# A gather's wait for TensorE's queries, at every third group of edges instead of every second

## The chip, the cores and the metric

The kernel runs on one core of one Trainium2 chip. The metric is device time in microseconds (us) of one execution: the median of several runs. Five engines work side by side, each on its own list of instructions: TensorE (PE in the profile; its weight loads are PEld), VectorE (DVE), ScalarE (ACT), GpSimd (POOL) and SyncE (SP). They wait for each other by semaphores: an instruction that is done raises a count, and another one waits until the count is high enough.

## The reference, cut to what matters

A graph has 12,500 nodes with 128 numbers each and 200,000 edges, in the order of their target node `dst`. Two convolutions with four heads follow a layer norm. In each, node projections give a query `q`, a key `k` and a value `v`, and then for all edges:

```
kj = k[src] + e
vj = v[src] + e
alpha = jnp.einsum('ehc,ehc->eh', q[dst], kj) / jnp.sqrt(...)
p = jnp.exp(alpha - amax[dst])
w = p / denom[dst]
out = jax.ops.segment_sum((vj * w[..., None]).reshape(-1, H * C), dst, num_segments=n)
```

A third stage multiplies gathered node rows by numbers of the edge and sums them by target. What matters here: an edge's key and value are fetched from the row of its source node, which lies anywhere, and its query comes from its target node, which lies close to that of the edge before.

## The kernel before, in words

**Work.** The edges are cut into 391 groups of 512 (4 tiles of 128). Each convolution runs over all groups, so 782 groups in all. `conv` (L775) writes the order out by hand: a loop over steps `s`, in which different parts of the work are done for different groups, and every engine gets its instructions in exactly that order.

**One step.** In step `s` the parts that matter are these, in the order of the code:

- `fetch_kv(s + 3)` (L814): GpSimd issues four indirect DMAs, one for each 128 edges, through `gather` (L597; the DMA itself is at L602). Each reads 128 rows of key and value (1 KB each) into the tile `kv`. There are 20 such tiles (`LAG + KVS`). Nothing else runs on GpSimd in the convolutions.
- `turn(s + 2)` and `keep_sums` (ScalarE: tile `OT` at L850 and L852; the sums `acc` at L867).
- `messages` and `sum_up` for a group 15 steps back (VectorE L839 and L840; TensorE L862 and L860). `messages` is the last reader of that group's `kv` tile.
- `scores(s)` (VectorE L883, L885 and L887): it multiplies TensorE's queries, tile `pq`, by the keys in `kv`.
- `query(s + 1)` (TensorE, L823): eight matmul instructions (four in the code) into two banks of `pq`. Four banks rotate, and the node work takes some of the same banks in between.

So each engine can run ahead of the others only as far as these buffers let it. TensorE's query of a group needs banks that `scores` of an earlier group has read; `scores` needs TensorE's result for its own group.

**The wait.** The first of a group's four gathers may get one more wait, by `gather`'s argument `behind`: it waits until the last matmul of `query(g - 3)` has raised TensorE's semaphore. `asked[g - 3]` holds that matmul. The data doesn't need it. In the code before, every odd group has this wait, 194 groups of each convolution (there is no `asked` for a negative number). All other waits of a gather are about data: the `kv` tile must have been read (`messages` of group g - 20), and the gather eight places earlier must have landed.

The third stage has gathers of its own (tile `hg`, the same L602) with a wait of its own kind; it isn't part of the change.

Of the kernel before, what the change touches and what calls it, by code (L numbers as in the profile page):

```python
# [533 lines left out]
def sorted_path(ctx: ExitStack, tc: tile.TileContext, sh_: Shared, x, edge_attr, out):  # L534
# [33 lines left out]
    kv_d, q_d, s1_d = sh_.kv_d, sh_.q_d, sh_.s1_d  # L568
# [30 lines left out]
    def gather(t, rows, g, behind=None):  # L599

        for u in range(U):
            i = nc.gpsimd.indirect_dma_start(  # L602
                out=t[:, u, :], out_offset=None, in_=rows[:, :],
                in_offset=bass.IndirectOffsetOnAxis(ap=srcI[:, g * U + u:g * U + u + 1], axis=0))
            if behind is not None and u == 0:
                tc.add_manual_dep(i.ins, behind.ins.name, mybir.DependencyInfo(
                    mybir.DependencyClass.Sync, mybir.DependencyReason.DATA), reason="a pause for TensorE's results")
# [169 lines left out]
    def conv(li):  # L777
# [8 lines left out]
        pps, outs, msgs, pas, asked = {}, {}, {}, {}, {}  # L786
# [4 lines left out]
        qws, kvs, Os, OTs, pqs, ALs, segs, accs, bst = {}, {}, {}, {}, {}, {}, {}, {}, {}  # L791
# [22 lines left out]

        def fetch_kv(g):
            kvs[g] = pool.tile([P, U, 2 * D], F32, name="kv", bufs=LAG + KVS)
            gather(kvs[g], kv_d[li], g, asked.get(g - 3) if g % 2 else None)

        def query(g):
            pqs[g] = [bank().rearrange("p (u c) -> p u c", u=2) for _ in range(U // 2)]  # L820
# [191 lines left out]
        with tc.manual_schedule():  # L1012
            for s in range(-AHEAD, last):
# [34 lines left out]
                if 0 <= s + 3 < NGR:  # L1048
                    fetch_kv(s + 3)
# [624 lines left out]
```

## Time and profile before

| what | value |
|---|---|
| median of 3 runs | 7359.88 us (7340.25 to 7360.03) |
| the profiled execution | 7424.75 us; its span, first to last instruction, 7422.9 us |
| granted TensorE clock, mean | 0.792 of full speed |
| first convolution, first gather to last message | 137.5 to about 2568 us |
| second convolution | about 2594 to 5030 us |
| third stage | 5057 us to the end |
| POOL busy in the span | 4867.4 us (66%) |
| PE, DVE, ACT busy | 5031.8 (68%), 4923.4 (66%), 3053.5 (41%) us |
| mean share of the 16 DMA engines, 700 to 2300 us | 0.56 to 0.63 |
| issues of `kv` gathers | 3128 (782 groups of 4) |

The profile records when each instruction started and ended on its engine, and how long the engine stood idle before it. Of that idle time it says what ended it ("releaser"), as far as a semaphore's update was recorded. About a fifth of TensorE's updates are missing, so many waits end on "remote". The ends of matmuls are modelled, not observed. Four views are used here: the page of sums, the list of waits (who waited for whom, in total, number of times, longest), the instructions of one tile, and the timeline (instructions in order of their start).

### The profile page before, as it was taken

The numbers are of one execution on the slowest core, as the hardware profiler recorded it, in microseconds if no ns is written. First come the engines' busy times: TensorE is split into PE (matmuls) and PEld (weight loads), VectorE is DVE, ScalarE is ACT, GpSimd is POOL, SyncE is SP. The second block draws the span as 40 slices with busy tenths as digits, with TensorE's granted clock in tenths as the row PEclk, the third lists the DMA queues.
The fourth block names the chain that finished last, engine by engine and source line by source line (L and its number), as shares of the span: only waits on it lengthen the run. The fifth ranks groups of instructions, "written<-read, shape, count | busy, mean of one in ns | idle before, by whom it ended". The sixth has DMA issues, their size and how long they took to land.

```text
span 7422.9 us, 89199 instructions
## 1 busy us (share of the span) xinstructions
PE 5031.8 (68%) x21249; PEld 3219.3 (43%) x21250; DVE 4923.4 (66%) x13362; ACT 3053.5 (41%) x7785; POOL 4867.4 (66%) x4779
## 2 busy tenths in 40 slices
PE   5566666666777646665666666665777787777777
PEld 4454555555555444444454545452233333333332
DVE  5566666777777746666676777774566666666666
ACT  3333333333333223333444444443555555555554
POOL 6676667676666367767666776654566666666664
PEclk8677777787777867777777777777888888888888
DMA  6455555566666445555555555544455555555554
GB/s 186 135 149 150 148 158 160 162 167 164 168 177 174 129 134 138 143 143 143 146 152 152 153 156 160 157 135 121 125 137 142 144 145 147 149 149 151 152 153 116
DMA packets 868134, 1107.31 MB, mean 149 GB/s; under 512 B 143858, under 2 KB 631568, under 8 KB 867603
## 3 DMA queue, kind: packets, MB, share of 16 engines
q0 software_dynamic: 250240, 692.16, 34.6%
q1 hardware_dynamic: 615832, 408.51, 19.8%
q8 instruction: 176, 2.88, 0.2%
q14 instruction: 355, 2.91, 0.1%
q10 hardware_dynamic: 1531, 0.84, 0.0%
HBM read 935.35 MB, written 165.60 MB: 148 GB/s over the span
## 4 chain that ended last, share of the span: by engine, by line
PE 27%; DVE 22%; another core or an unknown queue 17%; issue 15%; POOL 7%; ACT 6%; DMA 3%; SPq 1%; DVEq 0%; POOLq 0%; ACTq 0%
PE pa L862 8%; PE pa L1171 7%; PE pq L823 6%; POOL kv L602 5%; DVE prod L883 3%; DVE msg L839 2%; ACT M L1147 2%; ACT off L1136 2%; PE pa L860 2%; DVE O L595 2%; POOL hg L602 2%; DVE AL L887 2%; DMA kv<-fkv,srcI 1%; DVE tops L970 1%
## 5 line engine op out<-in xcount | busy, mean ns | idle before, releaser
L602 POOL DMA_INDIRECT kv<-fkv,srcI x3128 | 3291.2, 1052 | 1540.4 <-issue 893.0
L602 POOL DMA_INDIRECT hg<-fhm,srcI x1564 | 1490.6, 953 | 904.6 <-issue 506.0
L1171 PE MATMUL pa<-M,O 128*128 128x512 f32 x3128 | 1608.3, 661 | 295.8 <-ACT M L1147 87.5
L862 PE MATMUL pa<-msg,O 128*128 128x136 f32 x6256 | 1424.7, 363 | 374.1 <-issue 135.2
L883 DVE TENSOR_TENSOR prod<-pq,kv 128x256 f32<-128x256 f32 x1564 | 648.2, 416 | 1333.6 <-remote 737.4
L862 PEld LDWEIGHTS pa<-msg,O 128*128 128x128 f32 x6256 | 1108.1, 244 | 770.0 <-issue 549.3
L823 PE MATMUL pq<-qw,OT 128*128 128x132 f32 x6256 | 1125.1, 332 | 430.0 <-remote 124.3
L823 PEld LDWEIGHTS pq<-qw,OT 128*128 128x128 f32 x6256 | 1034.8, 244 | 471.1 <-remote 207.1
L1171 PEld LDWEIGHTS pa<-M,O 128*128 128x128 f32 x3128 | 624.4, 210 | 1042.5 <-issue 659.0
L852 ACT ACTIVATE OT<-off,fone 128x512 f32<-128x512 f32 x782 | 564.5, 722 | 334.0 <-remote 210.3
L1175 DVE TENSOR_REDUCE acc<-pa 128x128 f32<-128x512 f32 x391 | 265.4, 679 | 603.3 <-remote 448.9
L867 ACT COPY acc<-pa 128x136 f32<-128x136 f32 x782 | 203.6, 261 | 998.1 <-remote 489.4
L850 ACT ACTIVATE off<-rows,fless 128x512 f32<-128x512 bf16 x782 | 560.5, 717 | 106.1 <-DMA rows<-rel_d 67.5
L1147 ACT ACTIVATE M<-hg,s 128x128 f32<-128x128 f32 x1564 | 495.7, 388 | 193.3 <-remote 141.9
L887 DVE TENSOR_REDUCE AL<-prod 128x16 f32<-128x528 f32 x782 | 549.6, 703 | 27.1
L839 DVE TENSOR_TENSOR msg<-kv,wt 128x512 f32<-128x512 f32 x782 | 531.8, 680 | 34.0 <-ACT wt L984 17.3
L595 DVE TENSOR_TENSOR O<-fiota,REL 128x512 f32<-128x512 f32 x782 | 532.2, 681 | 9.4 <-PE pa L862 9.4
L1136 ACT ACTIVATE off<-fiota,REL 128x128 f32<-128x128 f32 x1564 | 495.3, 387 | 0.6 <-ACT M L1147 0.2
L1138 ACT ACTIVATE O<-off,fone 128x512 f32<-128x512 f32 x391 | 282.2, 722 | 273.2 <-remote 226.7
L1158 DVE TENSOR_TENSOR M<-hg,sh 128x384 f32<-128x384 f32 x782 | 392.5, 539 | 0.0
L860 PE MATMUL pa<-msg,fCAR 128*1 128x136 f32 x1196 | 286.7, 329 | 0.0
L1123 ACT COPY d<-sh 128x32 f32<-128x32 f32 (+3 forms) x50 | 9.2, 185 | 647.7 <-remote 448.4
(238 smaller groups left out, 5102.7 us busy)
## 6 DMA issues: line engine op xcount, KB each, us to landing
rows<-rel_d SPq DMA_DIRECT2D x390, 256.0 KB
fsum<-acc SPq DMA_DIRECT2D x782, 68.0 KB
qw<-fq SPq DMA_DIRECT2D x782, 66.0 KB
kv<-fkv,srcI POOLq DMA_INDIRECT x3128
hg<-fhm,srcI POOLq DMA_INDIRECT x1564
fout<-acc SPq DMA_DIRECT2D x391, 64.0 KB
fhm<-qkv SPq DMA_DIRECT2D x98, 176.0 KB
A<-fsum SPq DMA_DIRECT2D x196, 68.0 KB
```

Source lines behind the costliest of these rows:

```text
L595: nc.vector.tensor_tensor(O, iob[:, None, :].to_broadcast([P, U, P]), REL[:, g * U:(g + 1) * U, None].to_broadcast([P, U, P]), op=OP.is_equal)
L602: i = nc.gpsimd.indirect_dma_start(out=t[:, u, :], out_offset=None, in_=rows[:, :], in_offset=bass.IndirectOffsetOnAxis(ap=srcI[:, g * U + ...
L823: asked[g] = nc.tensor.matmul(pqs[g][u // 2][:, u % 2, 0:QD], OT[:, u, :], qw, start=True, stop=True)
L839: nc.vector.tensor_mul(msg[:, :, :, 0:C], kv4(kv, D), wt[:, :, i, :, None].to_broadcast([P, U, H, C]))
L850: nc.scalar.activation(off, rows[g // RG][:, g % RG * GE:(g % RG + 1) * GE], AF.Abs, bias=sh_.less)
L852: nc.scalar.activation(OTs[g].rearrange("p u e -> p (u e)"), off, AF.Relu, bias=sh_.one, scale=-1.0)
L862: nc.tensor.matmul(pas[g], O[:, u, :], msg[:, u].rearrange("p h c -> p (h c)"), start=(u == 0), stop=(u == U - 1))
L883: nc.vector.tensor_mul(prod[:, c, :, 0:C], half[:, :, 0:D].rearrange("p u (h c) -> p u h c", h=H), kv4(kvs[g], 0)[:, c])
L887: nc.vector.tensor_reduce(ALs[j][:, :, i, :], prod, AX.X, OP.add)
L1136: nc.scalar.activation(off[:, u, :], iob, AF.Abs, bias=REL[:, g * U + u:g * U + u + 1], scale=-1.0)
L1147: nc.scalar.activation(M[:, u, 0, :], hg[:, u, 0:P], AF.Copy, scale=s0[:, i * U + u:i * U + u + 1])
L1171: summed[g] = nc.tensor.matmul(pas[g], O[:, u, :], M[:, u], start=(u == 0), stop=(u == U - 1))
```

## The change

One condition in `fetch_kv` is changed. The first gather of group g waits for the queries of group g - 3 where g is a multiple of 3, instead of where g is odd. That leaves 130 such waits in each convolution instead of 194. The order of the instructions on every engine is the same before and after; only the semaphore waits on GpSimd's list differ.

```
         def fetch_kv(g):
             kvs[g] = pool.tile([P, U, 2 * D], F32, name="kv", bufs=LAG + KVS)
-            gather(kvs[g], kv_d[li], g, asked.get(g - 3) if g % 2 else None)
+            gather(kvs[g], kv_d[li], g, asked.get(g - 3) if g % 3 == 0 else None)
```

## The prediction

> **What bounds the kernel now.** I read the page of sums first, for which engine is full.
>
> ```profile
> PE 5031.8 (68%) x21249; PEld 3219.3 (43%) x21250; DVE 4923.4 (66%) x13362; ACT 3053.5 (41%) x7785; POOL 4867.4 (66%) x4779
> ...
> L602 POOL DMA_INDIRECT kv<-fkv,srcI x3128 | 3291.2, 1052 | 1540.4 <-issue 893.0
> ...
> L883 DVE TENSOR_TENSOR prod<-pq,kv 128x256 f32<-128x256 f32 x1564 | 648.2, 416 | 1333.6 <-remote 737.4
> ```
>
> No engine is full. The gathers that the change touches take 1052 ns each, and 0.30 us lie between two of them (the "issue" gaps). Four make 4 x 1.052 + 4 x 0.30 = 5.41 us for a group. By the starts of the first gathers of groups 30 and 380, a group takes 6.07 us in either convolution. So GpSimd is some 0.66 us short of being the bound, and that rest is the wait which the change makes rarer.
>
> Next, whether anybody waits for the gathers. The view of the tile `kv` lists it at its end:
>
> ```profile
> who waited for it (us, times):
>   PE pa L862: 44.7, 38
>   DVE prod L883: 30.6, 10
>   PEld pa L862: 22.2, 20
> ```
>
> Hardly anybody. VectorE's `prod` waited for it 10 times in 782 groups. From the rows, a group's last gather ends 12.7 us (median) before `prod` reads it, and in 9 of 10 groups over 9.3 us. GpSimd has its data there early; making it earlier gains nothing by itself.
>
> Then the list of waits: who is waited for.
>
> ```profile
> DVE prod L883 <- remote: 737.4, 215, 15.9
> ...
> DVE prod L883 <- PE pq L823: 309.7, 185, 11.4
> POOL kv L602 <- remote: 253.1, 139, 4.5
> POOL kv L602 <- PE pq L823: 214.0, 88, 6.9
> ```
>
> `prod` waits for two things, `kv` (30.6 us, above) and TensorE's queries; so of these 1047 us nearly all, "remote" included, is TensorE's. GpSimd waits for TensorE in its two lines by 467 us. Yet TensorE is only 68% busy. The timeline shows what kind of wait this is:
>
> ```profile
> 1504.14 0.95 POOL L602 DMA_INDIRECT kv<-fkv,srcI  x1 [0.30 <-issue]
> ...
> 1504.44 0.50 PE L862 MATMUL pa<-msg,O 128*128 128x136 f32 x2
> ...
> 1504.78 0.61 PE L823 MATMUL pq<-qw,OT 128*128 128x132 f32 x4
> ...
> 1506.56 0.27 ACT L867 COPY acc<-pa 128x136 f32<-128x136 f32 x1 [5.87 <-PE pq L823]
> 1506.62 0.42 DVE L883 TENSOR_TENSOR prod<-pq,kv 128x256 f32<-128x256 f32 x1 [2.91 <-PE pq L823]
> ...
> 1506.91 0.95 POOL L602 DMA_INDIRECT kv<-fkv,srcI  x1 [1.81 <-PE pq L823]
> ```
>
> TensorE's last matmul ended at 1505.39. ScalarE, VectorE and GpSimd, which all waited for TensorE, started again together 1.2 to 1.5 us later. GpSimd had issued gathers without a break and stopped at 1505.09 to wait. This is the rule in the trace, not an accident. I call an idle time of over 0.45 us before a gather a pause. In the stretches 300 to 2300 and 2700 to 4700 us, pauses fill 12% of the time, but 1067 of TensorE's 2087 recorded semaphore updates (51%) fall into them; of VectorE's, 8%. The first update comes 1.19 us (median) after the pause begins, and the pause ends 0.38 us after that. So **while GpSimd issues gathers, TensorE's results reach the others late; a pause lets them out**. TensorE, VectorE and ScalarE form the loop that sets the pace, and what it waits for is such a release.
>
> One page speaks against this. The Trainium skill (Trainium Architecture — The Big Picture, section What this means for kernel authors) says that of the engines' ports only those shared by VectorE and GpSimd contend. By that rule the gathers could not hold TensorE up, nobody would depend on the pause, and the sum of this change would be 0. The 51% against 12% above, and the 1.2 us in the timeline, say otherwise; I go by them. The skill also says (Perfetto Trace Analysis, GPSIMD and Tensor rows of its instruction lifecycle) that a matmul's end is an estimate and its semaphore is raised only after the results are written; so it stays open whether results or only their semaphores are late, and the sum is the same either way.
>
> **What the change removes, adds and moves.** No instruction is added, removed or moved on any engine; 64 x 2 = 128 waits go (194 to 130 a convolution). Odd groups that are no multiple of 3 lose a wait, even multiples of 3 gain one. Behind a waiting gather stand only later gathers on GpSimd, and for those nobody waits (above), so the added waits cost nothing directly.
>
> The other waits of a gather don't take over. `messages` of group g - 20 ended at least 7.4 us before the gather that reuses its tile started; GpSimd can get ahead by one group more, 5.4 us. The gather eight places earlier had landed 6.2 us or more before. Both stay covered; were they not, GpSimd would pause there instead, which costs what a pause costs.
>
> So the cost lies in the pace of the loop. I counted the groups whose `prod` started (halves counted as halves), by the time since GpSimd's last pause ended, in the two stretches above:
>
> - first 6 us after a pause: 338.5 groups in 1526 us, 0.222 a us
> - 6 to 11 us: 119.5 in 1171 us, 0.102
> - 11 to 16 us: 34.5 in 331 us, 0.104; later 32 in 417 us, 0.077
> - in a pause: 134 in 490 us, 0.273
>
> A run of n groups without a pause keeps GpSimd busy 5.41n - 0.30 us. Its first 6 us bring 6 x 0.222 = 1.33 groups, the rest about 0.10 a us, and the pause p must bring what is missing to n, at 0.273 a us. As a test: today's waits find TensorE done already in a quarter of the cases, so that 257 pauses in 4000 us make a mean run of 4000 / 257 / 6.07 = 2.56, say 2.6 groups. It gives 13.77 us busy, 1.33 + 0.78 = 2.11 groups, p = 0.49 / 0.273 = 1.81 us, or (13.77 + 1.81) / 2.6 = 5.99 us a group. Measured: p 1.91, 6.07 a group. Good to 0.1 us.
>
> For runs of 3, the shortest that the change leaves: 15.93 us busy, 1.33 + 0.99 = 2.32 groups, p = 0.68 / 0.273 = 2.5 us, (15.93 + 2.5) / 3 = 6.14 us a group. That is 0.15 over the 5.99 of the same sum for today. **0.15 x 782 groups = +117 us.** If one in seven of the new waits is passed without a pause, runs are 3.5 groups, p = 3.3 us and the group 6.27: +0.28 x 782 = +219 us. I take the first, since late progress in a run that is now cut off by a pause, with results ready and waiting, should be a little better than in those that ran on. The third stage and the preparation don't change.
>
> The sum is against the profiled execution: 7425 + 117 = 7542. That one is 65 us above the median of the runs, so on the median: 7360 + 117 = **7477 us**, say 7475.
>
> **The rivals.**
>
> *The pause stays as short as it is (faster).* After runs of just 2 groups (200 of them) the pause is 1.61 us: 1.19 until the updates come, then the restart. In 8 of 10 pauses the query waited for had ended, by the rows, before the pause began, about 3 us before. So the loop may have room, and the time lost is that of stopping GpSimd. With p = 1.61 after three groups: (15.93 + 1.61) / 3 = 5.85 us a group, -0.22 x 782 = -172: 7188 us. Against it: the third group's query needs its own release on the way, and progress late in a run is 0.10 a us where 1 / 6.07 = 0.165 is needed.
>
> *Nothing comes of it.* Runs of 4 happen today where a wait was passed (59 of them); the pause after them is 2.83 us. Halfway between 1.61 and 2.83 lies 2.22: (15.93 + 2.22) / 3 = 6.05, -0.02 x 782 = -16 us: 7344. For it: runs of 2 and of 4 both take about 6.07 a group. Against it: the runs of 4 are those in which TensorE was early, so for runs not chosen that way the pause should be longer.
>
> *The loop comes to a stand in the third group (much slower).* If the late progress, for lack of free `pq` banks, is that of the last row, 0.077 a us: 1.33 + 0.76 = 2.09 groups, p = 0.91 / 0.273 = 3.3 us, (15.93 + 3.3) / 3 = 6.41 a group, +0.42 x 782 = +328: 7688. It decides where the group's second pair of banks needs `scores` of the group just before, which happens when the node work takes a bank in between. The 0.104 at 11 to 16 us, which is where a run of 3 ends, is against it.
>
> **How the numbers follow.** Forecast and its neighbours (up to +240 us): 0.50. Much slower: 0.07. Nothing: 0.16. Faster: 0.27. What a measurement here can tell from no change is 0.3%, 22 us. So slower 0.57, the same 0.16, faster 0.27. The range reaches from 7270, halfway into the faster case (a part of its 0.27 lies below), up to 7600 (+240, just above the +219): about 2 in 10 stay out. The likeliest case's own range is 7400 to 7600.
>
> **What would show it.** Right: some 220 to 260 pauses of about 2.5 us before `kv` gathers in place of today's 269 (of 352 waits, in groups 31 to 382) of 1.6 to 2.8; more idle time in front of `prod` than 1333.6 us; the busy time of PE, DVE and POOL as before. Wrong: pauses still near 1.6 us, and less idle time before `prod` (the faster rival). If TensorE's updates no longer gather in the pauses, the whole reasoning is wrong.

## The result, and the profile after

The changed kernel takes **7552.99 us** (median of 6 runs, 7512.46 to 7582.44) against 7359.95 (6 runs of before, 7340.25 to 7389.97): a ratio of **1.0254 [1.0232, 1.0276]**, 193 us slower. The forecast was 7475 us.

The two profiled executions lie closer together, 7549.6 against 7422.9 us of span. The stages tell where the difference sits:

| us | before | after | |
|---|---|---|---|
| first convolution, first gather to last message | 2430.8 | 2504.0 | +73 |
| second convolution | 2435.1 | 2526.8 | +92 |
| third stage, which the change doesn't touch | 2393.3 | 2351.1 | -42 |

So the convolutions lost 165 us. In all later profiles in which the kernel before takes about 7360 us, the third stage takes 2351 to 2387 us; before's 2393 was at the high end, as its whole profiled execution was 65 us above the median. That is most of what lies between the 127 us of the spans and the 193 us of the medians.

The page of sums of the changed kernel, the lines that answer to those of before:

```profile
PE 4992.7 (66%) x21249; PEld 3190.1 (42%) x21250; DVE 4922.7 (65%) x13362; ACT 3060.2 (41%) x7785; POOL 4871.9 (65%) x4779
...
L602 POOL DMA_INDIRECT kv<-fkv,srcI x3128 | 3296.1, 1054 | 1701.3 <-issue 922.5
...
L883 DVE TENSOR_TENSOR prod<-pq,kv 128x256 f32<-128x256 f32 x1564 | 648.1, 416 | 1509.4 <-remote 913.1
```

The work is the same: each engine is busy within 1% of before, a gather takes 1054 ns. What grew is idle time: 161 us more ahead of the gathers (1540.4 to 1701.3), 176 us more ahead of `prod` (1333.6 to 1509.4). Both are about the 165 us that the convolutions lost; by the prediction's account they are the same time, seen from two engines.

The list of waits of the changed kernel:

```profile
DVE prod L883 <- remote: 913.1, 217, 20.6
POOL kv L602 <- PE pq L823: 534.6, 116, 14.9
...
DVE prod L883 <- PE pq L823: 299.3, 203, 8.6
...
POOL kv L602 <- remote: 141.0, 71, 4.3
```

By its two lines ("remote" counted as TensorE's, as in the prediction) GpSimd waits for TensorE less often, 187 times instead of 227, and longer: 676 us instead of 467. The longest such wait rose from 6.9 to 14.9 us. One of the long ones, in the timeline of the changed kernel (start, duration, instruction, idle time before it):

```profile
1590.86 0.95 POOL L602 DMA_INDIRECT kv<-fkv,srcI  x1 [0.31 <-issue]
...
1593.59 0.42 DVE L883 TENSOR_TENSOR prod<-pq,kv 128x256 f32<-128x256 f32 x1 [5.67 <-remote]
...
1594.19 2.10 PE L823 MATMUL pq<-qw,OT 128*128 128x132 f32 x8 [3.80 <-remote]
...
1596.56 0.97 POOL L602 DMA_INDIRECT kv<-fkv,srcI  x1 [4.75 <-PE pq L823]
```

GpSimd stopped at 1591.81 to wait for a query. That query had not run. VectorE got TensorE's earlier results 1.8 us after the stop; only then could TensorE go on, ran the query from 1594.19 to 1596.29, and let GpSimd go. In the prediction's example the query was done, and the stop only had to let its result out. Here a whole turn of the loop had to fit into the stop.

Counted over groups 31 to 382 of both convolutions (704 groups; a pause is an idle time of over 0.45 us before a gather that has the wait):

| | waits | that stopped GpSimd | mean pause | query already ended at the stop, by the rows: share, mean pause | not ended: mean pause | us a group |
|---|---|---|---|---|---|---|
| before | 352 | 269 (76%) | 1.95 us | 81%, 1.68 us | 3.05 us | 6.07 |
| after | 234 | 188 (80%) | 3.44 us | 51%, 1.83 us | 5.13 us | 6.28 |

A stop at an ended query costs nearly what it did. The other kind costs two thirds more (5.13 against 3.05 us), and it went from one stop in five to one in two. The pauses also give the time: 704 / 188 = 3.74 groups lie between two stops, and four gathers with their gaps are 5.41 us, so 5.41 + (3.44 - 0.30) / 3.74 = 6.25 us a group. For before it is 5.41 + (1.95 - 0.30) / 2.62 = 6.04.

### The profile page after: what moved, and what is told of

Its sections match the earlier page's. It is cut to its first block, busy times and chain, and to the rows that moved or that the text cites. A ratio compares the mean times of both kernels' runs of the same rounds, so it can differ in the third digit from the quotient of the medians.

```text
span 7549.6 us, 89193 instructions
## 1 busy us (share of the span) xinstructions
PE 4992.7 (66%) x21249; PEld 3190.1 (42%) x21250; DVE 4922.7 (65%) x13362; ACT 3060.2 (41%) x7785; POOL 4871.9 (65%) x4779
## 4 chain that ended last, share of the span: by engine, by line
PE 28%; DVE 22%; another core or an unknown queue 17%; issue 16%; POOL 8%; ACT 3%; DMA 3%; SPq 1%; DVEq 0%; POOLq 0%; ACTq 0%
PE pa L1171 10%; PE pa L862 7%; POOL kv L602 7%; PE pq L823 5%; DVE prod L883 3%; DVE msg L839 2%; DVE O L595 2%; PE pa L860 2%; DVE AL L887 2%; DMA kv<-fkv,srcI 1%; DVE M L1158 1%; POOL hg L602 1%; DVE tops L970 1%; DVE top L909 1%
## 5 line engine op out<-in xcount | busy, mean ns | idle before, releaser
L602 POOL DMA_INDIRECT kv<-fkv,srcI x3128 | 3296.1, 1054 | 1701.3 <-issue 922.5
L862 PE MATMUL pa<-msg,O 128*128 128x136 f32 x6256 | 1403.7, 359 | 380.7 <-DVE msg L840 166.7
L883 DVE TENSOR_TENSOR prod<-pq,kv 128x256 f32<-128x256 f32 x1564 | 648.1, 416 | 1509.4 <-remote 913.1
L885 DVE TENSOR_TENSOR prod<-pq,EW 128x8 f32<-128x8 f32 x1564 | 247.0, 158 | 0.0
```

Of the source, the lines that this page charges most:

```text
L602: i = nc.gpsimd.indirect_dma_start(out=t[:, u, :], out_offset=None, in_=rows[:, :], in_offset=bass.IndirectOffsetOnAxis(ap=srcI[:, g * U + ...
L862: nc.tensor.matmul(pas[g], O[:, u, :], msg[:, u].rearrange("p h c -> p (h c)"), start=(u == 0), stop=(u == U - 1))
L883: nc.vector.tensor_mul(prod[:, c, :, 0:C], half[:, :, 0:D].rearrange("p u (h c) -> p u h c", h=H), kv4(kvs[g], 0)[:, c])
```

## The experiments

Theory: in the convolutions TensorE's results reach the others late while GpSimd issues gathers; a stop lets them out; rarer waits stop GpSimd later relative to TensorE. Rivals: a stop only costs GpSimd's time (then no wait at all is best); the number of waits is of no account; it matters which groups wait (odd, even, which remainder).

All edits are against the kernel before, and each comparison is with runs of the kernel before on the same chip at the same time. One thing must be said first, since no number can be read without it: **the kernel before itself took 6579 to 6592 us in three of the sets of runs and 7364 to 7420 us in four**, with the same code. I call them the 6580 and the 7360 condition; the result above belongs to the second. Times are compared only inside a set.

### No wait, every group, even groups, every fourth group (6580 condition)

The call in `fetch_kv`, its last argument in the four kernels:

```
-            gather(kvs[g], kv_d[li], g, asked.get(g - 3) if g % 2 else None)
+            gather(kvs[g], kv_d[li], g, None)
+            gather(kvs[g], kv_d[li], g, asked.get(g - 3))
+            gather(kvs[g], kv_d[li], g, asked.get(g - 3) if g % 2 == 0 else None)
+            gather(kvs[g], kv_d[li], g, asked.get(g - 3) if g % 4 == 3 else None)
```

> No kv gather waits for queries any more; only the waits for data are left (the kv tile read by messages of group g - 20, and landings). Theory (TensorE's results come out late while GpSimd issues, a pause lets them out): GpSimd runs ahead until the kv tiles are all in use and then pauses for messages, later than today; progress late in a run is 0.09 to 0.10 groups a us, so a group takes 6.4 to 6.8 us, 7600 to 7950 us in all, slower than the change. Rival A (the time is lost by stopping GpSimd, no result is held): GpSimd's own 5.41 us a group become the pace, 7360 - 0.66 x 782 = 6850 us. Rival B (the waits hardly matter, the change's slowdown is a matter of which groups wait): within 1% of before, 7290 to 7430.

> Every kv gather group waits for the queries three groups back. Theory: a run of one group is 5.1 us, in which the first-six-us rate of 0.22 a us already brings more than the one group needed, so many waits are passed at once; where one blocks, the pause is at least 1.5 us. Between 5.41 (none blocks) and 6.7 us a group (all block); I expect 6.0 to 6.3, 7300 to 7550 us, with more and shorter pauses than before. Rival A (stopping GpSimd costs the time): clearly slower than before, towards 6.7 us a group, 7850 us. Rival C (fewer waits is worse all the way): faster than before by as much as the change is slower, 7170 us.

> As before, but the even groups wait instead of the odd ones: the number of waits is that of before. Theory: only the distance of the pauses counts, 7360 us within 0.6% (7315 to 7405). Rival B (it matters which groups wait, since batches of 8 groups and rows of 2 groups repeat with an even period, which a distance of 3 runs across): differs from before by over 1%.

> Every fourth group waits (3, 7, 11, ...), which keeps to the odd groups of before. Theory: runs of 4 or more are 21.3 us busy, 1.33 + 1.53 = 2.86 groups of 4, the pause 4.2 us or more: at least 6.38 us a group, +0.3 to +0.5 against before, 7600 to 7750 us, slower than the change's 7553. Rival B (odd groups are the right ones, and 3 was bad for its parity): 7360 to 7450 us, faster than the change. Rival A: faster than before, (21.3 + 1.6) / 4 = 5.74 us a group, 7100 us.

Measured, beside 6578.52 us of the kernel before (31 runs):

| kernel | us | ratio |
|---|---|---|
| no wait | 6577.21 | 0.9993 [0.9983, 1.0003] |
| every group | 6582.70 | 1.0004 [0.9994, 1.0013] |
| even groups | 6578.85 | 1.0000 [0.9990, 1.0009] |
| every fourth | 6580.06 | 1.0002 [0.9993, 1.0012] |

All four expectations were worked out for a kernel before of some 7360 us, and no account of that time fits this as it stands: here the waits do nothing. The profile of the kernel without waits shows why, in the chain that ended last, the groups and the waits:

```profile
POOL 29%; DMA 26%; DVE 18%; issue 17%; PE 4%; ACT 3%; SPq 1%; DVEq 0%; POOLq 0%; ACTq 0%
...
L602 POOL DMA_INDIRECT kv<-fkv,srcI x3128 | 3335.0, 1066 | 1038.0 <-issue 874.2
...
L883 DVE TENSOR_TENSOR prod<-pq,kv 128x256 f32<-128x256 f32 x1564 | 652.0, 418 | 928.0 <-DMA kv<-fkv,srcI 766.9
```

The gathers run almost without a break, a group takes 5.53 and 5.47 us, about the 5.41 that four gathers need, and `prod` waits for `kv` to land (766.9 us) and hardly for TensorE. GpSimd is the bound. In the kernel with waits at the even groups a query had always ended at least 5.6 us before the gather that names it, so that no wait stops anything. TensorE isn't held up here: in the two stretches of the prediction's counts, each of its 2761 recorded updates in the kernel without waits comes within 40 ns of the end of a TensorE row that carries one. In the trace of before, 1636 of 2087 come over 100 ns after the latest such end, and half of the 2087 over 1 us.

So what the prediction read from the trace of before belongs to the 7360 condition, and not to the code. The four runs are void as a test of the theory.

### The same two beside a pause without a wait (6580 condition again)

No wait and every group once more, and a third kernel that has no wait but lets GpSimd fill a small tile ten times, without waiting for anyone, where the wait stood (`idle` is a tile of 128 x 64 that nothing reads):

```
+            if g % 2 and g > 2:
+                for _ in range(10):
+                    nc.gpsimd.memset(idle, 0.0)
+            gather(kvs[g], kv_d[li], g, None)
```

> The kernel of e1_none again (no kv gather waits for queries), meant for a chip on which before takes about 7360 us. Theory there: GpSimd runs until its 20 kv tiles are in use and then pauses for messages; late progress 0.09 to 0.10 groups a us; 6.4 to 6.8 us a group, 7600 to 7950 us, slower than the change. Rival A (stopping GpSimd costs the time): 6850 us. Rival B (what counts is which groups wait): 7290 to 7430 us. On a chip where before takes about 6579 all agree on a ratio of 1.000.

> The kernel of e2_every again (every group waits for the queries three groups back), meant for a chip on which before takes about 7360 us. Theory there: a pause is over sooner the more often it comes; between 5.41 and 6.7 us a group, I expect 6.0 to 6.3, 7300 to 7550 us. Rival A: 6.7 us a group, 7850 us. Rival C (the more waits the better, linearly): 7170 us. On a chip where before takes about 6579: 1.000.

> No kv gather waits for queries; instead GpSimd fills a small scratch tile ten times (some 1.5 us of its own work, no DMA) ahead of each odd group's gathers from group 3 on. It is always there, whether TensorE is late or not. Theory, if what holds TensorE's results is the issuing of gathers: they come out in these stretches, and a group takes (10.8 + 1.5) / 2 = 6.2 us, bound by GpSimd: 7430 to 7500 us on a chip where before takes about 7360. Theory, if any work of GpSimd holds them: as none_b with more work, over 7700. On a chip where before takes about 6579, GpSimd is the bound and this adds 388 x 1.5 = 580 us: 7160 us, ratio 1.09.

Another chip, the same condition: 6591.99 us without waits (0.9998 [0.9989, 1.0008]) and 6594.06 with all (1.0002 [0.9992, 1.0012]), beside 6592.03. With the fills 7325.61, 1.1119 [1.1100, 1.1137]. Where GpSimd is the bound, its fills are simply added: 6.45 and 6.42 us a group, where the kernel without waits took 5.53 and 5.47. The expected ratio was 1.09; ten fills with the gaps around them cost 734 / 388 = 1.9 us and not 1.5. So the rival that a stop costs GpSimd's time holds in this condition, for a stop that really happens.

### The change once more (7360 condition)

> The changed kernel once more, without an edit. The four runs so far came from a chip on which before takes 6579 us instead of 7360, no wait for the queries ever blocks and GpSimd issues without a pause. Theory (what the wait costs or gains is there only where TensorE's results come out late): ratio 1.025 on a chip where before takes about 7360, and 1.000 within 0.2% on one where it takes about 6579. Rival (the change costs something of its own, such as a worse order): 1.02 on either.

7533.08 us beside 7363.77: **1.0232 [1.0206, 1.0257]**. The convolutions take 151 us more than before's, of 234 waits 191 stop GpSimd for 3.22 us each, and at 54% of the stops the query had ended. The result repeats with the condition, on a chip that had shown the other condition before (chip 4 by its number in both). The rival of this run, a cost of the change in either condition, isn't refuted by it, since the changed kernel itself never ran in the 6580 condition; the four kernels that change the same argument lost nothing there.

### No wait at all (7360 condition)

> No kv gather waits for queries, once more, in a call of its own, since both calls with several kernels met a machine on which before takes 6579 to 6592 us and GpSimd is the bound. If before takes about 7360 us here: theory 7600 to 7950 us, slower than the change; rival A (stopping GpSimd costs the time) 6850 us; rival B (what counts is which groups wait) 7290 to 7430 us. If before takes about 6590: ratio 1.000.

7951.33 us beside 7374.08: **1.0766 [1.0735, 1.0797]**, the largest loss, at the upper edge of the expected 7600 to 7950 us. A group takes 6.73 and 6.84 us. Its groups and then its waits:

```profile
L602 POOL DMA_INDIRECT kv<-fkv,srcI x3128 | 3249.2, 1039 | 2148.1 <-DVE msg L840 1141.5
...
L883 DVE TENSOR_TENSOR prod<-pq,kv 128x256 f32<-128x256 f32 x1564 | 647.9, 416 | 1983.0 <-remote 1381.5
```

```profile
DVE prod L883 <- remote: 1381.5, 234, 14.4
POOL kv L602 <- DVE msg L840: 1141.5, 207, 38.4
```

GpSimd now runs ahead until all 20 `kv` tiles are full, and then stops for `messages`, 158 pauses of 5.85 us in the stretches 300 to 2300 and 2700 to 4700 us, 23% of the time. In them lie 41% of TensorE's updates; the first comes 1.8 us after the stop, and 4.6 us more go by until the tile is free; it seems that the work must come down the whole loop first. A wait for the query is thus not what holds GpSimd back: without it another one does, later and longer. By the rival that stops only cost, this kernel would have been the best, 7360 - (6.07 - 5.41) x 782 = 6844 us, a ratio of 0.93. It is refuted here, and so is "no difference".

### A wait at every group (7360 condition)

> Every group's first kv gather waits for the queries three groups back, in a call of its own, for a machine on which before takes about 7370 us. No waits gave 1.077 and every third 1.023 to 1.025 there. Theory: runs of one group end inside the good first six us after a pause, so many waits are passed at once and few are short of 1.5 us; 6.0 to 6.3 us a group, ratio 0.99 to 1.025. Rival A (each pause costs its 1.5 us): 6.7 us a group, ratio 1.065. Rival C (the more waits the better, in line with 1.077, 1.025, 1): 0.975.

7287.25 us beside 7365.30: **0.9898 [0.9872, 0.9925]**, 1% faster than the kernel before. Its groups:

```profile
L602 POOL DMA_INDIRECT kv<-fkv,srcI x3128 | 3325.0, 1063 | 1403.1 <-issue 905.0
...
L883 DVE TENSOR_TENSOR prod<-pq,kv 128x256 f32<-128x256 f32 x1564 | 648.5, 417 | 1252.2 <-remote 540.6
```

There are 704 waits in the groups counted above, but only 243 of them stop GpSimd (35%), for 1.61 us each: fewer stops than before's 269, and shorter ones. At 86% of the stops (and 95% of all waits) the query had ended. The idle time before `prod` falls to 1252.2 us. A wait that comes early enough finds TensorE just behind, and lets out what is ready; one that comes late finds it a turn behind. The measured ratio lies at the lower edge of the expected 0.99 to 1.025. The rival that every pause costs its time (1.065) is refuted, and the gain is less than half of what "the more waits the better" promised (0.975).

The series is monotone: none 1.077, every third 1.023 to 1.025, every second 1, every 0.990.

### The pause without a wait (7360 condition)

> The kernel of blind_pause (no waits for queries; GpSimd fills a scratch tile ten times ahead of each odd group's gathers, some 1.9 us by the 734 us that it added in 388 places where GpSimd was the bound), in a call of its own, for a machine on which before takes about 7370 us. If the issuing of gathers is what holds TensorE's results: they come out in these stretches, GpSimd is then about the bound, (10.8 + 1.9) / 2 = 6.35 us a group, ratio 1.02 to 1.04, and TensorE's updates gather in the stretches of fills. If any work of GpSimd holds them and only idling lets them out: slower than no wait at all (1.077), since GpSimd works more, 1.08 to 1.13, and the updates avoid the fills.

7679.35 us beside 7419.70: 1.0338 [1.0309, 1.0367], against 1.0766 without waits and without fills. The groups of GpSimd and the wait of `prod` (the lines stand four further down):

```profile
L602 POOL DMA_INDIRECT kv<-fkv,srcI x3128 | 3170.1, 1013 | 1141.6 <-issue 989.5 <-DVE prod L889 82.7 <-DVE msg L844 14.4
...
L820 POOL MEMSET idle<- 128x64 f32 x3880 | 597.8, 154 | 199.9
```

```profile
DVE prod L887 <- DMA kv<-fkv,srcI: 1205.2, 640, 6.5
```

GpSimd is nearly full: per group 4 x 1.013 us of gathers, 1141.6 / 782 = 1.46 idle before them, (597.8 + 199.9) / 782 = 1.02 for the fills, 6.53 together, where 6.44 was measured. And `prod` waits for `kv` (1205.2 us, 640 times), as it does in the 6580 condition, and little for TensorE (137.5 us). TensorE's updates gather in these stretches, as expected: 39% of the recorded ones fall into the 20% of the time between the gathers around the fills, against 18% in the same kernel in the 6580 condition. So the fills took the place of the waits, and the rival that any work of GpSimd holds the results (1.08 to 1.13) is refuted: it is enough that GpSimd issues no gathers for some 2.6 us every second group, 1.5 of them filled with other work. Added to the kernel without waits, work that nobody needs made it faster. The Trainium skill (Trainium Architecture — The Big Picture, section What this means for kernel authors) lets only VectorE and GpSimd contend on the engines' side of the SBUF; these runs, which differ in no work of TensorE or VectorE, show a hold-up that this rule doesn't cover. The rule is about data, and what is late may be the semaphores alone (below).

### Key and value without an indirect gather (6580 condition)

Is it the issuing on GpSimd, or is it the transfers? Here SyncE fetches 512 consecutive rows a group; the lookup by source is left out, and GpSimd has nothing to do in the convolutions.

```
-            gather(kvs[g], kv_d[li], g, asked.get(g - 3) if g % 2 else None)
+            a = g * GE % (N - GE)
+            nc.sync.dma_start(kvs[g], kv_d[li][a:a + GE, :].rearrange("(u p) c -> p u c", p=P))
```

> In the convolutions the four gathers of a group are replaced by one plain DMA from SyncE's queue, which fills the same kv tile with the same bytes from consecutive rows of the same table (rows of other nodes than the edges' sources, so this leaves the lookup by source out). GpSimd has nothing to do there and no wait for queries is left. In a call of its own, for a machine on which before takes about 7370 us. If GpSimd's issuing of gathers holds TensorE's results: they come out at once, and the loop runs at its own pace, bounded below by VectorE's 4.2 busy us a group (2743 of 4000 us at 6.07 a group), say 4.4 to 5.3, ratio 0.83 to 0.92. If the transfers themselves hold them (the same bytes still move): about 6.0 us a group or more, ratio 0.98 to 1.05.

5945.66 us beside 6582.17: 0.9032 [0.9017, 0.9048]. In the 6580 condition the gathers are the bound, and they cost, issuing on GpSimd, lookup and scattered rows together, some 640 us. `prod` now waits for next to nothing, in the groups by line:

```profile
L884 DVE TENSOR_TENSOR prod<-pq,kv 128x256 f32<-128x256 f32 x1564 | 642.9, 414 | 113.8 <-PE pq L824 96.2 <-DMA kv<-fkv 10.9 <-DMA qw<-fq 3.0
```

Of the 113.8 us idle before it, 96.2 are TensorE's. But the question was about the other condition, which didn't come up, so it stays open.

## Why the prediction was right, and where it was off

- **What bounds the kernel**: right in the 7360 condition. TensorE's loop sets the pace, GpSimd's stops let its results out; after the change 46% of TensorE's updates lie in the 15% of time in pauses. The kernels without waits and with fills show by edits, not only by counting, that stopping the gathers is what counts. The prediction's 51% is of recorded updates; 2585 rows of TensorE in these stretches carry one, and even if all that are missing came outside a pause, 1067 of 2585 (41%) would lie in 12% of the time, where 8% of the rows end. VectorE's 8% says less, as 1994 of its 4886 are recorded.
- **No engine does more work, and the added waits cost nothing directly**: right. Busy times are within 1%, and `prod` waited for `kv` 21 times, 37.3 us in all.
- **The other waits of a gather don't take over**: right for every third group (GpSimd's waits for `messages` don't show among its larger ones). They do take over when all waits go.
- **The term that was mis-sized is the length of a run.** The forecast took runs of 3 groups, "the shortest that the change leaves", with p = 2.5 us and 6.14 us a group: +117 us. Measured: of 234 waits 46 passed without a stop, one in five, so runs are 3.74 groups, p = 3.44, the group 6.28, and the convolutions +165 us in the profile. The prediction's other sum, for one in seven passed, said 3.5 groups, 3.3 us, 6.27 and +219. In length, pause and pace it was the nearer one, and today's quarter of passed waits, which stood in the same text, was the reason to take it.
- **The base of both sums, and luck.** Both differences are taken from the sum's own 5.99 us for today, 0.08 under the measured 6.07, which alone makes 63 us of either. From 6.07 the two sums give +55 and +156 us; 165 was measured. So a run that was too short and a base that was too low offset each other, and that 7475 came within 78 us of 7553 is in part luck. The faster rival and "nothing" were priced from 6.07, the forecast and the slower rival from 5.99.
- **Why the first was taken**: "late progress in a run that is now cut off by a pause" should be better. It was: 0.168 groups a us at 6 to 11 us after a pause (before 0.102), 0.114 at 11 to 16 (0.104). It didn't make up for the longer runs, with 0.090 at 16 to 30 us.
- **Signs**: more idle time before `prod`, seen; pauses of about 2.5 us, too short; 220 to 260 pauses, too many (188), both for the same reason.
- **The faster rival** took the pause as 1.61 us, because in 8 of 10 pauses the query had ended before. That share was a result of the waits' spacing: it is 51% at every third group and 86% at every group. A stop at an ended query still costs 1.83 us, nearly the rival's price, but there are too few of them.
- **The much slower rival**, a stand in the third group, is wrong: p of 3.3 us was about right, but per 3.74 groups.

What stays open: what sets the condition; whether TensorE's results or only their semaphores are late; whether the issuing or the transfers hold them.

The second question the traces lean on without settling it. In the trace of before, 544 of the 2086 intervals between TensorE's recorded updates are under 60 ns, but only 29 of 2584 between the ends of the rows that carry them (in the kernel without waits, in the 6580 condition, 21 of 2760 intervals between updates). Updates that come out so close together look like semaphores kept back after their matmuls had run; the rows' ends are modelled, so this is no proof.

As to the third, the fills stop both: the skill (Perfetto Trace Analysis, section DMA Instruction — SWDGE (GPSIMD)) says that a gather's row ends with the last descriptor, and not with the data. The traces agree, since `prod` waits for a landing long after rows of 1.07 us have ended (766.9 us of such waits, above), so rows alone can't part the two. The transfers' own records lean to the issuing: of before's pauses in which an update of TensorE is recorded, 78% have the first one ahead of the last packet of the gather before the stop (medians 1.19 and 1.66 us after the stop), with fills 72%, without waits 51%. No edit shows it.

Even groups against odd ones never ran in the 7360 condition, and neither did every fourth; the monotone series speaks against a matter of odd and even, but it wasn't tried.

## What to carry to other kernels

A wait that the data doesn't need can still carry the pace: look at what comes free while an engine stands still, and count updates, not busy time, beside the rows that should carry them, as many may be missing. Before you make such a wait rarer, count how many of today's waits pass without a stop and carry that share into the length of a run; if waits that find nothing to wait for are free, as here, put them at every group (worth 1% in the one condition and nothing in the other). And before you read a rule of the chip from one trace, see whether the kernel before repeats its own time on other runs: here a whole mechanism came and went with the condition.

## What was not expected of the hardware

The same kernel takes 6579 to 6592 us or 7360 to 7420 us by the medians, and nothing between, in seven sets of runs and the first one; one chip, by its number, showed both. The mean granted clock goes with it, 0.85 to 0.86 in the kernels of some 6580 us against 0.77 to 0.80 in those of the other condition, but which follows which isn't shown. In the convolutions the clock alone doesn't make updates late: the kernel with the fills has 0.74 to 0.76 in the two stretches in both conditions, and 676 of TensorE's 1656 recorded updates come over 100 ns after a row's end in the 7360 condition, none of 2397 in the other. The third stage, without any of these waits, takes 2027 to 2033 us in the one and 2351 to 2393 in the other. The kernel with the fills takes the same 6.4 us a group in both conditions, since GpSimd is its bound in both; its 365 us of difference in span (7318.4 and 7683.1) lies nearly all in the third stage.

The profile's own record goes with the condition, too. Of the updates that VectorE's, ScalarE's and TensorE's rows carry, the trace of before has 45%, 47% and 78%; every trace of the 6580 condition has over 99% of each. So whether VectorE's and ScalarE's semaphores come late as well can't be read from the 7360 traces. Every time here comes with a recorded span and clock, so no run shows whether the condition, and with it the hold-up, would be there without the recording.
